# Layer 1's attention sums: the copy of W2's extra columns moved four rounds later in VectorE's order

## The chip, the cores and the metric

The kernel runs on one NeuronCore of a Trainium2 chip. The metric is the device time of one execution in microseconds (us). Before the change it is 1989.29 us, the median of three runs that took 1989.29, 1989.85 and 1982.86 us.

Names of engines: TensorE (PE in the profile, PEld for its weight loads), VectorE (DVE), ScalarE (ACT), GpSimd (POOL) and SyncE (SP). SyncE only issues DMA transfers here. GpSimd issues the indirect ones, which gather rows by a list of indices.

## What is computed

A pre-norm graph attention network with two layers on 3125 nodes of 768 values and 53125 edges (25000 drawn pairs in both directions and a loop at each node, sorted by destination). Layer 1 has 4 heads of 256 columns, layer 2 one head of 768. Cut to what matters:

```python
def gat_conv(x, edge_index, W, a_src, a_dst, bias, heads, out_ch, concat):
    xl = (x @ W).reshape(n, heads, out_ch)
    alpha_src = jnp.einsum('nhc,hc->nh', xl, a_src)
    alpha_dst = jnp.einsum('nhc,hc->nh', xl, a_dst)
    e = jax.nn.leaky_relu(alpha_src[src] + alpha_dst[dst], 0.2)
    m = jax.ops.segment_max(e, dst, num_segments=n)
    e = jnp.exp(e - m[dst])
    s = jax.ops.segment_sum(e, dst, num_segments=n)
    alpha = e / (s[dst] + 1e-16)
    out = jax.ops.segment_sum(xl[src] * alpha[:, :, None], dst, num_segments=n)
    ...
h0 = relu(layernorm(x))
h1 = relu(layer_norm(gat_conv(h0, W1, ...), g1, be1)) + (h0 @ Wr1 + br1)
h  = layer_norm(gat_conv(h1, W2, ...), g2, be2) + (h1 @ Wr2 + br2)
return x + h
```

## The kernel before

**Blocks.** The nodes are cut into 25 blocks of 128 destinations. The sorted edges of a block fill 17 tiles of 128 edges. A tile belongs to one or two quarters (32 destinations each) of its block.

**Layer 1's sums** (the function `sums`, called at the end of the stage with `first()` as an argument) compute the segment sum of messages. For each tile GpSimd gathers the 128 source rows of 1024 values from the DRAM table into a buffer `g` (L779, 512 KB), of which there are 13. VectorE makes the tile's weights `w` by two instructions: `oh`, a one-hot matrix of the destinations (L805), and `w`, that matrix times the attention factor of each head (L806). There are 9 buffers of the narrow `w` and 3 of the wide one. TensorE multiplies `w` by `g` into `pa` (L826).

**Rounds.** The 17 tiles of a block are taken in five rounds, 0 to 4, of 4, 4, 3, 3 and 3 tiles (three of these tiles lie in two quarters and have wide weights, so that every round is 16 products; the trace records each fp32 product twice, so a round is 32 records of L826). While TensorE works on a round, the gathers and weights of the next one are issued (`fetch`). After each round `step` runs once. It lets each generator in hand go one step further, up to its next `yield`: first `first()`, then the closing steps of finished blocks (`finish` and `end1`), then `more`, which fills gaps in TensorE's order with the residual products of later blocks (L1191, h0 times Wr1).

**The order.** PE, ACT and DVE run in the order in which this Python code emits their instructions (`manual_schedule`); GpSimd and SyncE have orders of their own. Every engine works through its instructions in order, so an instruction that waits holds all behind it.

**`first()`** closes the attention factors while the sums already run. `totals` transposes the factors, takes their running sums (the scan, L637), transposes back into `scr`, and stores the result to DRAM as `alo_d` (L642, 1700 KB, on SyncE's queue). Then `first()` takes a tile `w2` for layer 2's weights. It has the tag "W", as `scr` has, so it is the same memory, and whatever writes `w2` waits until the store has read `scr`. Eight transfers (L1214) bring W2 into columns 0 to 767 of `w2`, and a copy on VectorE (L1215) puts the two extra columns there: `wa2`, W2 times a_src2 and a_dst2, made long before. The names in the profile: w for `w2`, wa2s for `wa2`.

**Who else waits for the store.** Closing a block needs the totals of its last edges. They are fetched from `alo_d` by GpSimd (`ask`, L761, into `ao`), for block 0 behind the first gather of block 1's round 3, and for block 1 two gathers later. `finish` of block 0 starts on VectorE with L746, which reads `ao`, and goes on to `z` (L753, L1228), its layer norm (L486 to L1232) and, on TensorE, the transposes of `z` (L1239). `w2` itself is first read by the products for layer 2's table (L1260).

Of the kernel before, what the change touches and what calls it, by code (L numbers as in the profile page):

```python
# [69 lines left out]
def in_order(  # L70
# [170 lines left out]
    def edge_list(ep, pe):  # L241
# [32 lines left out]
        cnt = ep.tile([Q, NQ + 3], F32, name="cnt")  # L274
        first = ep.tile([Q, 1], I32, name="first")
        nc.vector.tensor_scalar(first, d_i[:, 0:1], 5, None, op0=OP.logical_shift_right)
        mark = ep.tile([Q, 6], F32, name="marks")
        for i in range(3):
            nc.vector.tensor_scalar(mark[:, i:i + 1], first, float(i + 1), None, op0=OP.add)
# [351 lines left out]
    def totals(heads, al, alo, alo_d, keep, xs, pp, tag, bufs):  # L631

        to_rows, to_slots = rows_and_slots(heads, pp, tag, bufs)
        for i, _ in enumerate(to_rows(al, xs)):
            if i == 1:
                yield
        nc.vector.tensor_tensor_scan(xs, keep[:, :S], xs, 0.0, op0=OP.mult, op1=OP.add)  # L637
        yield
        for i, _ in enumerate(to_slots(xs, lambda js, p: nc.scalar.activation(alo[:, js, heads:, :], p, AF.Copy))):
            if i == 1:  # L640
                yield
        nc.sync.dma_start(alo_d.rearrange("(p r) c -> p r c", p=128), alo.rearrange("p j v b -> p j (v b)"))  # L642
# [199 lines left out]
    with tc.tile_pool(name="m1", bufs=1) as mp:  # L842
# [322 lines left out]
        with tc.tile_pool(name="w2", bufs=1, reuse_waits="tile") as wp, tc.tile_pool(name="e1", bufs=2, reuse_waits="tile") as ep, \  # L1165
# [42 lines left out]
            def first():  # L1208
                nonlocal w2
                yield from totals(H, al1, alo1, alo1_d, keep1, xs1, pp, "p2", 2)  # L1210
                yield
                w2 = mp.tile([128, NK2, R2], F32, tag="W", name="w2")
                for k in range(NK2):
                    nc.sync.dma_start(w2[:, k, :C2], W2[k * 128:(k + 1) * 128, :])  # L1214
                nc.vector.tensor_copy(w2[:, :, C2:], wa2)  # L1215

            def end1(b, z, share):
# [50 lines left out]
                store_rows(nc.sync, table2, b, row)  # L1268

            sums(H, C1, table1, al1, alo1_d, 13, 3, gp, ap, pp, end1, more, (2.5, 3.8, 0, 0, 0.9), first(), -6.3)  # L1270


# [595 lines left out]
```

## Time and profile before

| | us |
|---|---|
| runs, median (lowest to highest) | 1989.29 (1982.86 to 1989.85) |
| profiled execution, its own time | 1990.46 |
| span of the profiled execution, first to last instruction | 1988.6 |
| PE busy in the span | 1793.4 (90%) |
| DVE busy in the span | 1060.1 (53%) |
| POOL busy in the span | 902.0 (45%) |
| granted TensorE clock, mean | 0.957 of full speed |

Times inside the trace are us from the start of the span. A row of a timeline has the start, the duration, the engine, the line, the operation, what it writes and reads, and the count of merged records; the brackets at its end give the engine's idle time just before and what ended it. "issue" stands for idle time in which the profile shows nothing that was waited for. A row of a table by stretch has the stretch, its length, the busy time of PE, PEld, DVE, ACT and POOL with the count of instructions, the granted clock, the mean busy share of the 16 DMA engines, and GB/s.

### The profile page before, as it was taken

The page shows a single profiled execution, that of the slowest core. Times are in us where ns is not written, and L with a number is a line of the kernel's source. Part 1 is how long each engine was busy: PE and PEld are TensorE (multiplying, and loading weights), DVE is VectorE, ACT ScalarE, POOL GpSimd, SP SyncE. Part 2 cuts the span into 40 slices and gives each one's busy share as a digit, 9 for nine tenths or more (in the row PEclk, how much of TensorE's full clock was granted, in tenths as well). Part 3 has the DMA queues.
Part 4 walks back from the last instruction along what each step waited for, and adds up shares of the span by engine and source line. Part 5 has one row for each costly group of instructions (what it writes and reads, how often), then busy time and mean ns, then how long its engine had stood idle before and what let it go on. Part 6 is the DMA issues. An engine that isn't in the chain of part 4 may idle for free. (4 is left out here: it accounts for less than half of the span.)

```text
span 1988.6 us, 34126 instructions
## 1 busy us (share of the span) xinstructions
PE 1793.4 (90%) x12558; PEld 985.9 (50%) x12558; DVE 1060.1 (53%) x3030; ACT 295.5 (15%) x1094; POOL 902.0 (45%) x977
## 2 busy tenths in 40 slices
PE   8999999998779999999998998838989888998986
PEld 5666665664446555565544554534333333333332
DVE  7673437886645555655566454524444444444445
ACT  2122331001211221221111211101000000000000
POOL 2000101112455566566656653052666666666662
PEclk9999999998889999999999999858999998999999
DMA  7823448774699999999999996486999999999984
GB/s 244 267 96 132 129 144 205 177 176 152 229 408 352 386 375 396 381 381 408 391 392 367 376 362 264 142 286 207 338 327 327 328 328 325 330 338 323 341 284 147
DMA packets 180786, 574.86 MB, mean 289 GB/s; under 512 B 32768, under 2 KB 55034, under 8 KB 180485
## 3 DMA queue, kind: packets, MB, share of 16 engines
q0 software_dynamic: 108432, 408.63, 57.5%
q1 hardware_dynamic: 67786, 153.57, 22.5%
q10 hardware_dynamic: 4394, 10.39, 1.3%
q8 instruction: 103, 1.69, 0.3%
q14 instruction: 71, 0.57, 0.1%
HBM read 503.27 MB, written 73.85 MB: 290 GB/s over the span
## 5 line engine op out<-in xcount | busy, mean ns | idle before, releaser
L779 POOL DMA_INDIRECT g<-table,idx_s x832 | 816.3, 981 | 555.6 <-issue 208.6
L826 PE MATMUL pa<-g,w 128*32 128x256 f32 (+2 forms) x5868 | 527.9, 429 | 69.5 <-issue 52.6
L826 PEld LDWEIGHTS pa<-g,w 128*32 128x32 f32 x5868 | 204.5, 111 | 360.8 <-issue 238.2
L1326 PE MATMUL pr<-wr,h 128*128 128x384 f32 (+1 forms) x800 | 299.2, 509 | 26.7 <-issue 26.3
L1260 PE MATMUL p<-w,h1T 128*128 128x384 f32 (+2 forms) x800 | 280.3, 497 | 5.2 <-DVE h1T L1246 2.6
L801 DVE TENSOR_SCALAR w<-iota_f,rel_s,al 128x32 f32<-128x32 f32 (+1 forms) x416 | 102.3, 318 | 264.1 <-PE pa L826 156.1
L1326 PEld LDWEIGHTS pr<-wr,h 128*128 128x128 f32 (+1 forms) x800 | 143.7, 190 | 182.1 <-issue 112.6
L1260 PEld LDWEIGHTS p<-w,h1T 128*128 128x128 f32 (+1 forms) x800 | 143.9, 187 | 127.8 <-issue 34.1
L806 DVE TENSOR_TENSOR w<-oh,al 128x128 f32<-128x128 f32 (+1 forms) x416 | 131.8, 317 | 124.8 <-PE pa L826 54.0
L931 PE MATMUL pm<-w,h0l 128*128 128x344 f32 (+1 forms) x468 | 144.2, 463 | 0.0
L1191 PE MATMUL pr<-h0k,wr 128*128 128x256 f32 (+1 forms) x576 | 141.8, 392 | 2.4 <-issue 2.2
L1068 PE MATMUL pm<-h0g,wr 128*128 128x512 f32 x288 | 134.2, 614 | 0.0
L931 PE MATMUL pm<-w,h0g 128*128 128x344 f32 x432 | 130.0, 456 | 0.3 <-ACT h0g L910 0.3
L1191 PEld LDWEIGHTS pr<-h0k,wr 128*128 128x128 f32 x576 | 106.3, 190 | 33.4 <-issue 13.0
L999 POOL DMA_DIRECT2D hot_d<-ohd x25 | 13.5, 540 | 222.7 <-DVE own L503 126.6
L805 DVE TENSOR_SCALAR oh<-iota_f,rel_s 128x32 f32<-128x32 f32 (+1 forms) x416 | 110.4, 265 | 0.5 <-issue 0.2
L492 ACT ACTIVATE bn_sd<-bn_mv,eps 128x1 f32<-128x1 f32 (+1 forms) x50 | 14.7, 294 | 638.6 <-DVE bn_mv L488 445.3
L931 PEld LDWEIGHTS pm<-w,h0l 128*128 128x128 f32 (+1 forms) x468 | 86.6, 189 | 45.7 <-issue 8.4
L931 PEld LDWEIGHTS pm<-w,h0g 128*128 128x128 f32 x432 | 81.4, 192 | 40.3 <-issue 0.9
L1068 PEld LDWEIGHTS pm<-h0g,wr 128*128 128x128 f32 x288 | 54.4, 197 | 58.0 <-issue 57.9
L552 PE MATMUL pq<-tabs,hot 128*128 128x25 bf16 x1275 | 41.7, 180 | 39.4 <-issue 35.5
L1244 ACT ACTIVATE h1T<-p,be_c,g_c 128x128 f32<-128x128 f32 (+1 forms) x200 | 72.0, 476 | 18.3 <-PE p L1239 12.6
(306 smaller groups left out, 1439.5 us busy)
## 6 DMA issues: line engine op xcount, KB each, us to landing
s<-slo_d SPq DMA_DIRECT2D x25, 544.0 KB
g<-table,idx_s POOLq DMA_INDIRECT x832
table<-row SPq DMA_DIRECT2D x24, 512.0 KB
own<-table SPq DMA_DIRECT2D x24, 512.0 KB
h1T_d<-h1T SPq DMA_DIRECT2D x24, 512.0 KB
h<-h1T_d SPq DMA_DIRECT2D x22, 512.0 KB
ring<-in_x_dram SPq DMA_DIRECT2D x24, 384.0 KB
table<-row SPq DMA_DIRECT2D x24, 384.0 KB
```

Source lines behind the costliest of these rows:

```text
L552: nc.tensor.matmul(q[:, j], oh[:P, o:o + 128], tabs[:, i], start=(i == 0), stop=(i == 2))
L779: nc.gpsimd.indirect_dma_start(out=g[:, :width], out_offset=None, in_=table[:, :], in_offset=bass.IndirectOffsetOnAxis(ap=idx_s[:, b * J + ...
L801: nc.vector.tensor_scalar(w[:, 0, :], iota_f[:, lo:hi], rel_s[:, c:c + 1], al[:, POS[j], 0, b:b + 1], op0=OP.is_equal, op1=OP.mult)
L805: nc.vector.tensor_scalar(oh, iota_f[:, lo:hi], rel_s[:, c:c + 1], None, op0=OP.is_equal)
L806: nc.vector.tensor_tensor(w, oh[:, None, :].to_broadcast([128, heads, hi - lo]), al[:, POS[j], :, b:b + 1].to_broadcast([128, heads, hi - ...
L826: nc.tensor.matmul(pa[32 * q:32 * q + 32, o // f, o % f:o % f + m], w[:, o // cols, :], g[:, o:o + m], start=to not in opened, stop=False, ...
L931: nc.tensor.matmul(pm[:r, :C], h0[b][:, k, :], w1[:, k, i * C:(i + 1) * C], start=(k == 0), stop=(k == NK1 - 1))
L1068: nc.tensor.matmul(pm, wr1[:, k, m * 128:(m + 1) * 128], groups[gi][:, k, :], start=(k == 0), stop=(k == NK1 - 1))
L1191: nc.tensor.matmul(pm[:, :n], wr1[:, k, m * 128:(m + 1) * 128], loaded[i, k][:, :n], start=(k == 0), stop=(k == NK1 - 1))
L1244: nc.scalar.activation(hT[:, k0 + k, :r], pt[:, k, :r], AF.Relu, bias=be1_c[:, k0 + k:k0 + k + 1], scale=g1_c[:, k0 + k:k0 + k + 1])
L1260: nc.tensor.matmul(pm[:, :n], hT[:, k, :r], w2[:, k, o:o + n], start=(k == 0), stop=(k == NK2 - 1))
L1326: nc.tensor.matmul(pm[:, :384], h1[:, k, :r], wr2[:, k, i * 384:(i + 1) * 384], start=(k == 0), stop=False)
```

## The change

`first()` yields four times between the loads of W2 and the copy:

```diff
                 for k in range(NK2):
                     nc.sync.dma_start(w2[:, k, :C2], W2[k * 128:(k + 1) * 128, :])
+                for _ in range(4):
+                    yield
                 nc.vector.tensor_copy(w2[:, :, C2:], wa2)
```

Since `first()` goes one step a round, the copy is emitted four rounds later. No engine but VectorE has another order, and the loads of W2 stay where they are on SyncE's queue. From the copy on, lines have numbers higher by 2, and the running numbers of the tiles `g` and `w` are lower by 1 between the two places.

VectorE's order before, at both places (`w_4678` is the last weight of block 1's round 0, `w_4711` the first of round 1, `w_4854` and `w_4860` the last two of round 4; L746 begins the closing of block 0; DMAHW5 is the semaphore of the store to `alo_d`):

```order
L806 TENSOR_TENSOR w_4678<-oh,al_120 128x128 [waits DVE_49,PE_49]
L1215 COPY w_4682<-wa2s 128x8x2 [waits DMAHW5_49,Activation_49]
L805 TENSOR_SCALAR oh<-iota_f,rel_s 128x32
L806 TENSOR_TENSOR w_4711<-oh,al_120 128x128 [waits DVE_49]
...
L806 TENSOR_TENSOR w_4854<-oh,al_120 128x128 [waits DVE_49,PE_49]
L805 TENSOR_SCALAR oh<-iota_f,rel_s 128x64
L806 TENSOR_TENSOR w_4860<-oh,al_120 128x256 [waits DVE_49]
L746 TENSOR_SCALAR aw<-ao,has 128x4 [waits DMASW4_49]
```

The same places in VectorE's order of the changed kernel:

```order
L806 TENSOR_TENSOR w_4678<-oh,al_120 128x128 [waits DVE_49,PE_49]
L805 TENSOR_SCALAR oh<-iota_f,rel_s 128x32
L806 TENSOR_TENSOR w_4710<-oh,al_120 128x128 [waits DVE_49,PE_49]
...
L806 TENSOR_TENSOR w_4853<-oh,al_120 128x128 [waits DVE_49,PE_49]
L805 TENSOR_SCALAR oh<-iota_f,rel_s 128x64
L806 TENSOR_TENSOR w_4859<-oh,al_120 128x256 [waits DVE_49]
L1217 COPY w_4682<-wa2s 128x8x2 [waits DMAHW5_49,Activation_49]
L746 TENSOR_SCALAR aw<-ao,has 128x4 [waits DMASW4_49]
```

The copy went behind the thirteen pairs L805 and L806 that make the weights of rounds 1 to 4 of block 1, and stands right ahead of block 0's closing. Its waits are the same.

GpSimd's order, which the change leaves as it is but for the tiles' numbers, here as the changed kernel has it (`g_4728` is the last gather of round 1, the next three are round 2, `g_4807`, `g_4815` and `g_4821` are round 3, `g_4845` begins round 4):

```order
L779 DMA g_4728<-table_64,idx_s 128x1024 [waits DMASW7_49,PE_49]
L779 DMA g_4761<-table_64,idx_s 128x1024 [waits DMASW0_49,PE_49]
L779 DMA g_4767<-table_64,idx_s 128x1024 [waits DMASW1_49,PE_49]
L779 DMA g_4773<-table_64,idx_s 128x1024 [waits DMASW2_49,PE_49]
L779 DMA g_4807<-table_64,idx_s 128x1024 [waits DMASW3_49,PE_49]
L761 DMA ao<-alo_d,at_last 128x200 [waits DMAHW5_49,DMASW4_49]
L779 DMA g_4815<-table_64,idx_s 128x1024 [waits DMASW5_49,PE_49]
L779 DMA g_4821<-table_64,idx_s 128x1024 [waits DMASW6_49,PE_49]
L761 DMA ao<-alo_d,at_last 128x200 [waits DMASW7_49]
L779 DMA g_4845<-table_64,idx_s 128x1024 [waits DMASW0_49,PE_49]
```

The first L761, of block 0, waits for the store to `alo_d` as the copy does, in both kernels.

## The prediction

> **What bounds the kernel now.** I began with the page, to see whether TensorE is the engine whose idle time counts, and then went to the place of the change with the view of who waited for whom, the timelines of the engines and a table of busy time by stretch. The page, whose second view cuts the span into 40 slices of 49.7 us:
>
> ```profile
> span 1988.6 us, 34126 instructions
> PE   8999999998779999999998998838989888998986
> PEclk9999999998889999999999999858999998999999
> DMA  7823448774699999999999996486999999999984
> ```
>
> TensorE is busy nine tenths of nearly every slice. Layer 1's sums start in slice 11 (about 520 us), and from there to about 1200 us the DMA engines are as full as TensorE is. The copy stands at 556 us, at the start of this stage. The waits between 520 and 640 us (us in total, times, longest):
>
> ```profile
> DVE w L1215 <- DMA alo_d<-scr: 14.7, 1, 14.7
> POOL ao L761 <- DMA alo_d<-scr: 7.7, 1, 7.7
> PE pa L826 <- DVE w L806: 6.6, 1, 6.6
> ```
>
> These three lines are the case. VectorE stands 14.7 us at the copy, until the store of scr to alo_d has read its buffer. Behind the copy stand weights w, and TensorE waits 6.6 us for the first of them. But GpSimd waits for the same store, at ask (L761), and what is queued there are the gathers g of the same sums. The change touches the first wait alone. So the question is what else TensorE would have waited for. The table by stretch (PE, PEld, DVE, ACT and POOL busy, then PEclk, DMA share, GB/s):
>
> ```profile
> 541.70:556.40 14.70, 7.46 (x68) 4.38 (x63) 0.00 (x0) 1.44 (x4) 4.68 (x5) 0.89 1.02 411
> 556.40:577.00 20.60, 16.04 (x124) 9.28 (x128) 15.49 (x53) 2.20 (x4) 13.45 (x14) 0.83 1.03 403
> 600.00:620.00 20.00, 20.00 (x128) 13.51 (x127) 5.91 (x21) 2.76 (x10) 7.32 (x8) 1.00 0.93 349
> 620.00:900.00 280.00, 276.34 (x2250) 163.84 (x2248) 162.12 (x539) 54.80 (x158) 171.50 (x180) 1.00 1.00 381
> ```
>
> TensorE is idle 7.2 us of the first stretch and 4.6 us of the second, and then hardly at all: 0 of 20 us and 3.7 of 280 us. Time that it has gained by 600 us would reach the end, since nothing later has slack to lose it in. Before 600 us the DMA engines are full (1.02 and 1.03 at over 400 GB/s) while TensorE has gaps: there the transfers set the pace.
>
> **The change part by part.** It removes and adds no instruction. On VectorE, thirteen pairs of L805 and L806, the weights of block 1's rounds 1 to 4, come ahead of the copy. VectorE's rows (start, us, idle before in brackets):
>
> ```profile
> 556.42 0.18 DVE L1215 COPY w<-wa2s 128x16 f32<-128x16 f32 x1 [14.74 <-DMA alo_d<-scr]
> 567.09 0.29 DVE L806 TENSOR_TENSOR w<-oh,al 128x128 f32<-128x128 f32 x1 [3.45 <-PE pr L1191]
> 567.93 0.33 DVE L746 TENSOR_SCALAR aw<-ao,has 128x4 f32<-128x4 f32 x1
> 576.18 0.81 DVE L1232 TENSOR_SCALAR z<-z,bn_mv,bn_rs 128x1024 f32<-128x1024 f32 x1
> ```
>
> The 14.74 us go: VectorE can write the weights from 541.7 us on. Does the copy wait at its new place? The pair before the last ahead of it is the row at 567.09, which waits for TensorE to free its buffer, held by round 1's weights. In the trace it is let go with the end of the L1191 matmuls behind round 1. Even if these end some us earlier, that is after 556.4, so the copy finds the store done, and the new wait is nil. The copy's own 0.18 us and a start of about 0.2 now lie ahead of block 0's z. z is finished at 577.0, and its reader L1239 starts at 585.06 (below), so 8 us hide these 0.4; without that cover they would cost 0.4 us. Now TensorE:
>
> ```profile
> 530.36 3.64 PE L826 MATMUL pa<-g,w 128*32 128x256 f32 x32
> 545.90 2.12 PE L826 MATMUL pa<-g,w 128*32 128x256 f32 x26 [1.06 <-issue]
> 547.95 2.86 PE L1191 MATMUL pr<-h0k,wr 128*128 128x256 f32 x12
> 557.45 5.16 PE L826 MATMUL pa<-g,w 128*32 128x256 f32 x32 [6.65 <-DVE w L806]
> 562.54 4.15 PE L1191 MATMUL pr<-h0k,wr 128*128 128x256 f32 x16
> 566.62 4.23 PE L826 MATMUL pa<-g,w 128*32 128x256 f32 x38
> 576.70 1.51 PE L826 MATMUL pa<-g,w 128*32 128x256 f32 x23 [1.69 <-DMA g<-table,idx_s]
> 583.24 1.89 PE L826 MATMUL pa<-g,w 128*32 128x256 f32 x26 [0.69 <-DMA g<-table,idx_s]
> 585.06 1.09 PE L1239 MATMUL p<-ident,z 128*128 128x128 f32 x8
> 595.28 1.93 PE L826 MATMUL pa<-g,w 128*32 128x256 f32 x32
> ```
>
> A round of the sums is 32 records. Round 1 of block 1 starts at 557.45, 6.65 us after L1191 ended at 550.81, and takes 5.16 us, since the first weights come one by one and the clock is halved. Without the copy the weights are there. Are the gathers? GpSimd's rows and the one of SyncE's queue that stores alo_d:
>
> ```profile
> 536.51 0.99 POOL L779 DMA_INDIRECT g<-table,idx_s  x1 [0.30 <-PE p L582]
> 542.58 0.94 POOL L779 DMA_INDIRECT g<-table,idx_s  x1 [1.31 <-PE p L582]
> 548.48 0.94 POOL L779 DMA_INDIRECT g<-table,idx_s  x1 [0.30 <-issue]
> 557.07 0.95 POOL L761 DMA_INDIRECT ao<-alo_d,at_last  x1 [7.66 <-DMA alo_d<-scr]
> 559.57 0.98 POOL L779 DMA_INDIRECT g<-table,idx_s  x1 [0.30 <-issue]
> 564.64 0.93 POOL L779 DMA_INDIRECT g<-table,idx_s  x1 [0.30 <-issue]
> 567.33 0.94 POOL L779 DMA_INDIRECT g<-table,idx_s  x1 [1.76 <-PE pr L1191]
> 571.05 1.07 POOL L779 DMA_INDIRECT g<-table,idx_s  x1 [0.30 <-issue]
> 618.00 0.93 POOL L779 DMA_INDIRECT g<-table,idx_s  x1 [8.85 <-PE pa L826]
> ```
>
> ```profile
> 543.55 0.32 SPq L642 DMA_DIRECT2D alo_d<-scr  x1
> ```
>
> By GpSimd's order 542.58 is the last gather of round 1, 559.57 that of round 3, 564.64 that of round 4, and 571.05 that of block 2's round 0. TensorE's two waits on gathers give their time under way: 564.64 to 576.70 is 12.1 us, 571.05 to 583.24 is 12.2 us. The store, issued 1 us behind round 1's last gather, took until 556.4, 12.9 us. From below: round 0's last gather, 536.51, was used from 545.90 at the latest, 9.4 us. So round 1's last gather lands between 552.0 (9.4) and 555.5 (12.9), and I take 554.7 (12.1), because it shares the engines with the store. Most of TensorE's 6.65 us is therefore hidden by nothing but changes its cause: 3.9 us stay as a wait for gathers, and 2.8 us are gained (2.0 to 5.4). The round then goes at the pace of the row at 530.36, which has the halved clock too: 3.64 for 5.16 us, 1.5 gained. TensorE is some 4.3 us ahead behind round 1 (3.5 to 6.9).
>
> It keeps none of this. Round 3's last gather is issued at 559.57, behind ask, and lands at about 571.7. Round 4's is issued at 564.64 and lands at 576.7, as in the row. All of GpSimd's gaps between 557.07 and 564.64 are its own 0.30 us: it runs at its own pace from the moment at which the store is done, and the change doesn't move the store. TensorE arrives 4 us earlier at the same two landings and waits there. What remains is GpSimd's first gather of block 2, which takes over a buffer of round 1: it waited 1.76 us, where the fourth gaps elsewhere are 1.31, so 0.45 us of it is TensorE's. With the DMA engines full, an issue that comes 0.45 us earlier lands between 0 and 0.45 us earlier. I take 0.2, about the middle.
>
> Sum: 14.7 us on VectorE, of which 4.3 reach TensorE, less 4.3 given back at rounds 3 and 4, plus 0.2: 0.2 us, or 1988.4 for the span of 1988.6. The profiled execution was timed at 1990.46, 1.9 above its span and 1.2 above the median of 1989.29. Against the median this is 1989.1, and I say **1989.0 us**: no change.
>
> **The rivals.** *First, the gain stays.* If the gathers are in SBUF when TensorE asks, it gains the whole 6.65 us, and round 1 runs in the 1.93 us of the row at 595.28 instead of 5.16, 3.2 more: 9.9 us, or 1979.4. For it: the trace names the weights as what ended the wait, and TensorE is full from 600 us on, so that a gain would last; 618.00 shows GpSimd waiting for TensorE, no longer the reverse. Against it: two waits on gathers stand between the copy and that point, and both are set by issues behind ask.
>
> *Second, slower: the clock.* TensorE's granted clock falls after a pause. Stretches of 3.41 us, columns as above:
>
> ```profile
> 549.79:553.20 3.41, 1.01 (x5) 0.56 (x3) 0.00 (x0) 0.62 (x2) 0.00 (x0) 1.00 1.01 424
> 553.20:556.61 3.41, 0.00 (x0) 0.00 (x0) 0.18 (x1) 0.00 (x0) 0.00 (x0) 0.50 0.99 408
> 560.03:563.44 3.41, 3.41 (x24) 2.01 (x15) 2.96 (x12) 0.00 (x0) 2.50 (x4) 0.50 1.03 394
> 570.27:573.68 3.41, 1.92 (x18) 0.83 (x21) 3.38 (x9) 0.10 (x1) 1.73 (x3) 1.00 1.03 405
> ```
>
> After a stretch with 1.01 us of work it was 0.50, and it stayed there to the end of a full stretch, 10.2 us in all. Between 570.27 and 573.68 TensorE still had 1.92 us of work, and kept its clock. When it arrives 4 us earlier, that work may be done before, the pause gathers around 570 to 576, and a second halved stretch of up to 10.2 us begins at 573.7, over work that is now at full clock. It costs one slow round at least (3.64 less 1.93, 1.7 us) and half the stretch at most, 5.1 us; with 3 us, 1992.3. It decides from the point at which a whole stretch has about 1 us of work. Against it: up to 583 us TensorE waits for gathers anyway, and these pauses would take up most of the loss.
>
> The Trainium skill (TensorE: Matmul & The Clock Gate, What's actually happening) has the same mechanism: the clock is halved after an idle window of about 3.4 us, and given back after a busy one. By that rule the pause moved to 570 us would halve the clock again if it covers a window; the rows agree on the length of a window, and none shows the pause there.
>
> *Third, the change does not take the wait away*: VectorE reaches the copy before the store is done and stands there again. That needs the L1191 matmuls behind round 1 to end before 556.4. At the earliest they end at 550.81 plus 1.93 for the round plus 3.8 for their 16 records (12 took 2.86), 556.5, with every gather there. So there is nothing left to wait for even then, and if there were, it would lie in z's 8 us of slack: 1989.3.
>
> **How the numbers follow.** No lasting effect, third rival included: 0.70. Gain stays, wholly or in half: 0.18. A second halved stretch: 0.12. A measurement can tell about 0.5% (9.9 us) from no change. The first rival just reaches that at its full size, which takes half its chance; with something that these rows do not show, 0.12 for faster. The second stays under 5.1 us, so slower by 0.5% needs a cause that I don't see: 0.08. Same: 0.80. The likeliest case alone spans what the three runs spanned, 1982.9 to 1989.9, and 1 or 2 us around it. The range takes in the first rival nearly whole and the second whole (1989.3 and 5.1 is 1994.4): 1980 to 1995.
>
> **What would show it.** Right: the copy at about 563 to 567 us with no idle time before it; VectorE's weights for rounds 1 and 2 before 550 us; TensorE's first matmuls of round 1 near 551, with a wait on gathers inside the round instead of one on w; and the waits on gathers near 576.7 and 583.2 still at the same times, the one at 576.7 longer than 1.69 us. Wrong: those two landings come several us earlier, so that they hung on TensorE or VectorE after all; or TensorE reaches them with its gathers there; or the clock reads 0.50 after 570 us, and the rows behind 588 us are later than now.

## The result and the profile after

The changed kernel takes 1984.35 us (median of 17 runs, 1979.03 to 1990.21), the kernel before 1987.07 us in 17 runs. The ratio is 0.9985, with a 95% interval from 0.9973 to 0.9997. A later set with the same two kernels gave 1.0009 (0.9995 to 1.0023). Taken together that is no change.

The profiled span went from 1988.6 to 1983.7 us, 4.9 us less, and nothing of this comes from the change. Here is the scan L637, which stands ahead of the change in VectorE's order, before and after:

```profile
530.78 4.69 DVE L637 TENSOR_TENSOR_SCAN scr<-keep,scr 100x2176 f32<-100x2176 bf16 x1 [7.40 <-ACT scr L573]
```

```profile
525.88 4.70 DVE L637 TENSOR_TENSOR_SCAN scr<-keep,scr 100x2176 f32<-100x2176 bf16 x1 [7.24 <-ACT scr L573]
```

The later trace is 4.90 us ahead before the changed code begins. So all times below are compared from the scan on. I call *the segment* the time from the scan's start to the gather behind GpSimd's wait of about 9 us, where TensorE is the bound again and nothing has slack: 618.00 less 530.78 is **87.22 us** before, 613.35 less 525.88 is **87.47 us** after. The change gains nothing in the place where it acts.

Inside the segment much moved. VectorE after (start, us, idle before):

```profile
542.10 0.29 DVE L806 TENSOR_TENSOR w<-oh,al 128x128 f32<-128x128 f32 x1 [2.95 <-remote]
545.22 0.29 DVE L806 TENSOR_TENSOR w<-oh,al 128x128 f32<-128x128 f32 x1 [1.39 <-PE pr L1191]
554.83 0.30 DVE L806 TENSOR_TENSOR w<-oh,al 128x128 f32<-128x128 f32 x1 [6.91 <-issue]
555.67 0.17 DVE L1217 COPY w<-wa2s 128x16 f32<-128x16 f32 x1
558.64 0.29 DVE L746 TENSOR_SCALAR aw<-ao,has 128x4 f32<-128x4 f32 x1 [2.80 <-DMA ao<-alo_d,at_last]
```

The copy has no idle time before it; the 14.74 us are gone. VectorE now waits in these four other places, 14.05 us in all ("remote" stands for a releaser that the profile does not tell). The longest wait, 6.91 us, is at the weight that takes over the buffer of round 1's first weight; the row names no releaser, but in VectorE's order this instruction waits for TensorE. The 2.80 us are for the totals. TensorE after (the rows of rounds 1 to 4, and the two waits on gathers in block 2's round 0):

```profile
545.99 1.05 PE L826 MATMUL pa<-g,w 128*32 128x256 f32 x4
550.71 0.59 PE L826 MATMUL pa<-g,w 128*32 128x256 f32 x2 [3.67 <-DMA g<-table,idx_s]
552.02 3.29 PE L826 MATMUL pa<-g,w 128*32 128x256 f32 x26 [0.72 <-DMA g<-table,idx_s]
555.24 3.72 PE L1191 MATMUL pr<-h0k,wr 128*128 128x256 f32 x16
558.89 1.64 PE L826 MATMUL pa<-g,w 128*32 128x256 f32 x23
560.90 0.39 PE L826 MATMUL pa<-g,w 128*32 128x256 f32 x1 [0.37 <-issue]
563.00 0.38 PE L826 MATMUL pa<-g,w 128*32 128x256 f32 x1 [1.71 <-issue]
565.12 0.58 PE L826 MATMUL pa<-g,w 128*32 128x256 f32 x1 [1.75 <-issue]
566.56 0.59 PE L826 MATMUL pa<-g,w 128*32 128x256 f32 x1 [0.86 <-issue]
568.01 6.08 PE L826 MATMUL pa<-g,w 128*32 128x256 f32 x69 [0.86 <-issue]
577.11 0.59 PE L826 MATMUL pa<-g,w 128*32 128x256 f32 x2 [0.68 <-DMA g<-table,idx_s]
578.39 1.89 PE L826 MATMUL pa<-g,w 128*32 128x256 f32 x26 [0.69 <-DMA g<-table,idx_s]
```

Round 1 begins 20.1 us after the scan instead of 26.7. It does two of its products and stops, for gathers: the wait of 6.65 us on w has become 3.67 and 0.72 us on g. The round ends 29.4 us after the scan (552.02 and 3.29, less 525.88), before it was 31.8.

Round 2 starts at 33.0 us (558.89; before 35.8) and breaks up: behind 23 of its 32 records come five gaps, 5.55 us together, for which the profile names no cause ("issue"). At 42.1 us (568.01) five of its records are still to come, and the lead is gone; before, TensorE was six records into round 3 at 40.1 us (566.62 and 4.23, less 530.78). Then rounds 3 and 4 go in one row without a wait. At the last gather of block 2's round 0 TensorE is at 52.5 us (578.39) in both traces (583.24 before). GpSimd after:

```profile
537.66 0.94 POOL L779 DMA_INDIRECT g<-table,idx_s  x1 [1.27 <-remote]
552.30 0.95 POOL L761 DMA_INDIRECT ao<-alo_d,at_last  x1 [7.79 <-DMA alo_d<-scr]
559.79 0.94 POOL L779 DMA_INDIRECT g<-table,idx_s  x1 [0.30 <-issue]
561.04 0.94 POOL L779 DMA_INDIRECT g<-table,idx_s  x1 [0.31 <-DMA g<-table,idx_s]
568.87 0.93 POOL L779 DMA_INDIRECT g<-table,idx_s  x1 [3.14 <-PE pa L826]
613.35 0.94 POOL L779 DMA_INDIRECT g<-table,idx_s  x1 [8.75 <-PE pa L826]
```

It still waits for the store at ask. Block 2's first gather (561.04) comes 35.2 us after the scan instead of 36.6, and its fifth (568.87) waits 3.14 us for TensorE and is back at 43.0 us, where it was (42.7; 573.50 before). The table by stretch after, with columns as in the prediction:

```profile
556.40:577.00 20.60, 14.35 (x116) 8.65 (x114) 11.71 (x38) 2.21 (x4) 12.64 (x14) 0.83 1.03 405
565.10:571.90 6.80, 5.05 (x40) 3.40 (x42) 3.01 (x10) 2.21 (x4) 3.05 (x4) 0.50 1.03 407
```

The DMA engines are as full as before (1.03 at 405 GB/s). The last row shows something new: the clock was halved a second time, from 565.1 to 571.9 us, over the end of round 2 and the first half of the row at 568.01, which is about round 3.

### The profile page after: what moved, and what is told of

It is laid out like the page before. It is cut to its first block, busy times and chain, and to the rows that moved or that the text cites. A ratio compares the mean times of both kernels' runs of the same rounds, so it can differ in the third digit from the quotient of the medians.

```text
span 1983.7 us, 34129 instructions
## 1 busy us (share of the span) xinstructions
PE 1797.1 (91%) x12558; PEld 988.9 (50%) x12558; DVE 1057.3 (53%) x3030; ACT 297.0 (15%) x1094; POOL 900.2 (45%) x977
## 5 line engine op out<-in xcount | busy, mean ns | idle before, releaser
L801 DVE TENSOR_SCALAR w<-iota_f,rel_s,al 128x32 f32<-128x32 f32 (+1 forms) x416 | 101.9, 315 | 255.2 <-PE pa L826 159.4
L806 DVE TENSOR_TENSOR w<-oh,al 128x128 f32<-128x128 f32 (+1 forms) x416 | 131.6, 316 | 136.5 <-PE pa L826 55.5
L1191 PE MATMUL pr<-h0k,wr 128*128 128x256 f32 (+1 forms) x576 | 141.9, 391 | 2.5 <-issue 2.3
L1068 PE MATMUL pm<-h0g,wr 128*128 128x512 f32 x288 | 132.7, 609 | 0.0
L1191 PEld LDWEIGHTS pr<-h0k,wr 128*128 128x128 f32 x576 | 105.6, 190 | 34.1 <-issue 14.2
L805 DVE TENSOR_SCALAR oh<-iota_f,rel_s 128x32 f32<-128x32 f32 (+1 forms) x416 | 108.6, 261 | 0.4
L1068 PEld LDWEIGHTS pm<-h0g,wr 128*128 128x128 f32 x288 | 53.6, 194 | 57.8 <-issue 57.5
L554 DVE TENSOR_TENSOR scr<-pq,ohh 128x500 f32<-128x500 f32 x100 | 56.8, 597 | 27.1 <-PE pq L552 27.0
```

Of the source, the lines that this page charges most:

```text
L554: nc.vector.tensor_tensor(pick[:, j0:j0 + n], q, ohh[:, j0:j0 + n, None, :].to_broadcast([128, n, heads, NB]), OP.mult)
L801: nc.vector.tensor_scalar(w[:, 0, :], iota_f[:, lo:hi], rel_s[:, c:c + 1], al[:, POS[j], 0, b:b + 1], op0=OP.is_equal, op1=OP.mult)
L805: nc.vector.tensor_scalar(oh, iota_f[:, lo:hi], rel_s[:, c:c + 1], None, op0=OP.is_equal)
L806: nc.vector.tensor_tensor(w, oh[:, None, :].to_broadcast([128, heads, hi - lo]), al[:, POS[j], :, b:b + 1].to_broadcast([128, heads, hi - ...
L1068: nc.tensor.matmul(pm, wr1[:, k, m * 128:(m + 1) * 128], groups[gi][:, k, :], start=(k == 0), stop=(k == NK1 - 1))
L1191: nc.tensor.matmul(pm[:, :n], wr1[:, k, m * 128:(m + 1) * 128], loaded[i, k][:, :n], start=(k == 0), stop=(k == NK1 - 1))
```

## Experiments

The runs were made in three sets, each timed beside the kernel before. Before took 1985.99 us in the first set, 1836.44 in the second and 1972.69 in the third, so times are compared within a set only. The segment is a difference inside one trace and is compared across all; each one is from the start of L637 to the gather behind the wait of 7 to 11 us, two rows of the run's timelines. The third column is the mean busy share of the DMA engines in the segment, and GB/s.

| run | segment, us | DMA share, GB/s | ratio to before (95% interval) |
|---|---|---|---|
| before, after | 87.22, 87.47 | 1.02 401, 1.02 401 | 0.9985 (0.9973 to 0.9997) |
| after_again | 87.26 | 1.02 402 | 1.0009 (0.9995 to 1.0023) |
| before_again | 87.45 | 1.03 405 | 1.0000 (0.9987 to 1.0013) |
| ask_late_copy_late | 88.11 | 1.01 398 | 1.0010 (0.9992 to 1.0027) |
| ask_late_copy_old | 87.41 | 1.02 400 | 0.9993 (0.9979 to 1.0007) |
| loads_late | 87.32 | 1.02 396 | 1.0007 (0.9991 to 1.0024) |
| loads_twice | 97.13 | 1.02 400 | 1.0053 (1.0035 to 1.0072) |
| loads_half | 84.13 | 1.03 405 | 0.9991 (0.9978 to 1.0003) |
| loads_half_copy_old | 83.84 | 1.03 405 | 0.9970 (0.9955 to 0.9986) |
| old_wait0 | 87.89 | 1.02 399 | 0.9992 (0.9972 to 1.0012) |
| old_wait3 | 94.21 | 0.98 372 | 1.0043 (1.0025 to 1.0061) |
| old_wait7 | 101.64 | 0.90 345 | 1.0076 (1.0047 to 1.0106) |
| late_wait3 | 92.04 | 0.98 381 | 1.0014 (0.9993 to 1.0036) |

**Is there a gain at all?** The two kernels unaltered:

> The changed kernel once more, unaltered. The segment is the time from the start of the scan L637 to the gather behind GpSimd's wait of about 8.8 us, where TensorE is the bound again: 87.2 us in the profile before (530.78 to 618.00), 87.5 in the profile after (525.88 to 613.35). Theory (gathers behind ask set the pace, so the copy gives at most 0.5 us): segment 86.5 to 88, ratio to before 0.9990 to 1.0010. Rival (the copy's place is worth the 2.7 us between the medians): segment 84 to 86, ratio 0.998 to 0.999.

> The kernel before once more, unaltered, to see how far the segment (scan L637 to the gather behind GpSimd's wait of about 9 us) differs between executions of one kernel. Theory (the transfers set the segment's length): 86.7 to 87.9, as in the six traces so far (87.2 to 88.1). Rival (the copy's place counts and the traces met it by chance): a segment more than 1 us away from 87.3.

Four segments of the two kernels lie between 87.22 and 87.47, with the copy early in two of them and late in two. The rival, that the 2.7 us between the first medians are the copy's, falls: after_again has the other sign, and no segment is near 84 to 86.

**What holds the segment: the order behind ask, or the bytes?** First ask itself, with the copy late:

```diff
-                if heads > 1 and b == 1 and place == 11:
-                    ask(0)
-                if heads > 1 and b and place == (13 if tiles_of(b) == J else 5):
+                if heads > 1 and b == 1 and place == 16:
+                    ask(0)
+                    ask(1)
+                if heads > 1 and b > 1 and place == (13 if tiles_of(b) == J else 5):
                     ask(b)
```

> The changed kernel with both fetches of totals (ask of blocks 0 and 1) moved behind the last gather of block 1, so that no gather of rounds 3 and 4 stands behind the store in GpSimd's order. Theory (gathers behind ask set the pace): these gathers are issued about 7 us earlier, TensorE's waits in rounds 3 and 4 shrink, and the segment is 2 to 6 us shorter than after's 87.5; ratio 0.996 to 0.999. If the DMA engines rather than the issue hold the gathers, they land no earlier and the segment stays at 87 to 88. Rival (the copy's wait alone counted): segment as after, 87 to 88.

> The kernel before, copy at its old place, with both fetches of totals moved behind the last gather of block 1. Theory (two covers, each hides the other): the copy's wait of about 14 us stays and TensorE starts round 1 when the store is done, but finds the gathers of rounds 3 and 4 earlier: segment 1 to 4 us shorter than 87.2, and 1 to 4 us longer than with the copy late; ratio 0.998 to 1.000. Rival (the copy alone counts): segment 87 to 88, ratio 1.000.

With the copy late, round 3's last gather was issued at 550.55 and round 4's at 557.80, 20.90 and 28.15 us after the scan; after has them at 554.81 and 559.79, 28.93 and 33.91. So the issue did come 8.0 and 5.8 us earlier, and the segment did not get shorter (88.11); with the copy at its old place it was 87.41, where 1 to 4 us less than 87.2 were expected. Two rows of TensorE and one of VectorE tell where it went (with the copy late):

```profile
573.62 3.18 PE L827 MATMUL pa<-g,w 128*32 128x256 f32 x28 [1.69 <-DMA g<-table,idx_s]
580.60 3.29 PE L827 MATMUL pa<-g,w 128*32 128x256 f32 x29 [2.74 <-DVE oh L806]
574.18 0.29 DVE L746 TENSOR_SCALAR aw<-ao,has 128x4 f32<-128x4 f32 x1 [14.45 <-DMA ao<-alo_d,at_last]
```

TensorE still waits for the last gather of round 4, which now has been under way for 15.8 us (557.80 to 573.62) instead of some 12. It can go on at 44.0 us after the scan, before at 45.9: an issue 5.8 us earlier is worth about 2 us at the landing. Then TensorE waits 2.74 us for block 2's weights, since VectorE stood 14.45 us at the totals that are now fetched later. So my statement that the landings are set by the issues behind ask was at best half of it. And since moving ask brings this new wait, these two runs alone don't show whether the order or the bytes hold the segment.

Then the loads of W2, at the copy's new place and from ScalarE's queue:

```diff
+                for _ in range(4):
+                    yield
                 for k in range(NK2):
-                    nc.sync.dma_start(w2[:, k, :C2], W2[k * 128:(k + 1) * 128, :])
-                for _ in range(4):
-                    yield
+                    nc.scalar.dma_start(w2[:, k, :C2], W2[k * 128:(k + 1) * 128, :])
                 nc.vector.tensor_copy(w2[:, :, C2:], wa2)
```

> The changed kernel with the eight loads of W2 (3.1 MB, some 7.7 us of the DMA engines at 405 GB/s) issued from ScalarE's queue at the copy's new place instead of from SyncE's queue as soon as the store is done. Theory (the DMA engines are full, so what is queued ahead of the gathers decides when they land): gathers of rounds 3 and 4 land 3 to 7 us earlier though they are issued at the same time, and the segment is 2 to 6 us shorter than 87.5; ratio 0.996 to 0.999. If the issue behind ask decides alone, the segment stays at 87 to 88. Rival (copy alone): as after.

The queue's row and the stretch in which the loads were missing, from this run:

```profile
566.48 6.42 ACTq L1216 DMA_DIRECT2D w<-in_L_gnn_W_dram  x7
```

```profile
557.00:566.00 9.00, 5.33 (x36) 2.51 (x35) 7.06 (x22) 0.07 (x1) 6.52 (x7) 0.95 0.93 309
```

The loads moved by some 15 us on the segment's scale (the first of them, issued just ahead of this row, at 566.07, 40.3 us after the scan; in before it was at 556.46, 25.7 us). In their absence the DMA engines moved 309 GB/s instead of the 401 that after shows between the same times, with GpSimd only just issuing again behind ask; then the loads took their share later. The expected 2 to 6 us did not come. The same bytes still had to pass within the segment, which would explain it. To see that it is the bytes, their number was changed, up and down (both against the changed kernel):

```diff
-                for k in range(NK2):
+                for k in list(range(NK2)) * 2:
                     nc.sync.dma_start(w2[:, k, :C2], W2[k * 128:(k + 1) * 128, :])
```

> The changed kernel with the eight loads of W2 issued twice into the same tile: 3.1 MB more for the DMA engines in this place and nothing else. Theory (the bytes between the scan and layer 2's first products set the segment's length): at 405 GB/s 7.8 us more, some of which the 8.8 us wait of GpSimd at the end may take up, so segment 91 to 95.5 and ratio 1.002 to 1.004. Rival (GpSimd's issue behind ask sets it, at its own 1.24 us a gather): segment 87 to 88.5, ratio 1.000.

```diff
-                for k in range(NK2):
+                for k in range(NK2 // 2):
                     nc.sync.dma_start(w2[:, k, :C2], W2[k * 128:(k + 1) * 128, :])
                 for _ in range(4):
                     yield
+                for k in range(NK2 // 2, NK2):
+                    nc.scalar.activation(w2[:, k, :C2], wr1[:, k - NK2 // 2, :C2], AF.Copy)
```

> The changed kernel with only four of the eight loads of W2; the other half of the tile is filled by ScalarE from the weights Wr1 that lie in SBUF, so layer 2's table is computed with other weights. 1.57 MB fewer, 3.9 us of the DMA engines at 405 GB/s. Theory (bytes): segment 83.5 to 86, ratio 0.9980 to 0.9995. Rival (GpSimd's issue): 87 to 88.

> The kernel before (copy at its old place) with the same half of the loads of W2 and the same fill by ScalarE. If the transfers still cover the copy's wait: segment within 0.5 us of the run with half the loads and the copy late. If half the loads uncover it: 1 to 3 us longer than that run. Rival (GpSimd's issue decides both): both 87 to 88.

In the last of these runs the copy stands ahead of the four yields, at its old place. With half of the loads ScalarE fills the other half of `w2` from Wr1, so what layer 2 computes is other numbers with the same work. The gather that ends the segment with the loads twice, and with half of them (their scans start at 519.16 and 517.04):

```profile
616.29 0.94 POOL L779 DMA_INDIRECT g<-table,idx_s  x1 [8.87 <-PE pa L826]
```

```profile
601.17 0.94 POOL L779 DMA_INDIRECT g<-table,idx_s  x1 [8.80 <-PE pa L826]
```

3.1 MB more make the segment 9.7 us longer, 1.57 MB fewer make it 3.3 us shorter. Both are near the bytes' time at 405 GB/s, 7.8 and 3.9 us. The first is 1.9 us above it, and above the expected range. By the third column, times the segment, 38.9 MB passed with the loads twice, 35.4 in before_again of the same set: 0.3 MB more than the loads account for, at 400 instead of 405 GB/s, which makes up the 1.9 us. The share in that column is 1.01 to 1.03 in every run down to old_wait0: the DMA engines are full over nearly all of the segment, and its length follows the bytes. This settles what holds the segment: the bytes that must pass in it. With half the loads the copy's place is still worth nothing there: 83.84 us with the old place, 84.13 with the new one, though VectorE stood 16.31 us at the old one. The timed medians of these two differ by 3.9 us in favour of the old place (1829.94 and 1833.82); 0.3 us of this lies in the segment, and where the rest lies was not followed.

**How much cover has the old place?** In the last set VectorE was made to stand longer: one copy more, which reads two values of one of the loads and so waits for that load; what it writes is overwritten.

```diff
+                nc.vector.tensor_copy(w2[:, 0, C2:], w2[:, 0, :2])
                 nc.vector.tensor_copy(w2[:, :, C2:], wa2)
```

(with 3 and 7 for 0 in the next two runs, and 3 at the copy's new place, in the changed kernel, in the last).

> The kernel before with one more copy on VectorE ahead of the old one. It reads two values of the first of W2's eight loads and is then overwritten, so that VectorE stands at the old place until that load has landed, by my estimate some 6 us after the store. This lengthens the wait of 14.7 us that the change removes. Theory (the transfers give TensorE 7.9 us of slack between 556 and 600 us: 4.6 and 3.3 in the table by stretch): hidden, segment 87 to 88.5 (87.2 and 87.5 in the two traces of before). Rival (what VectorE waits there reaches the end): 6 us more, 93.

> The same with the fourth load, by estimate some 12 us after the store. Theory: beyond the 7.9 us of slack, so 3 to 6 us show: segment 90 to 93.5, ratio 1.0015 to 1.003. Rival (whatever VectorE waits there is hidden): 87 to 88.5.

> The same with the last load, by estimate some 20 us after the store. Theory: 10 to 14 us show: segment 97 to 102, ratio 1.005 to 1.008. Rival (hidden): 87 to 88.5.

> The changed kernel with the same extra copy on the fourth load, so the wait stands at the copy's new place. Theory: the weights of rounds 1 to 4 are ahead of it, block 0's z has some 8 us of slack, so it is hidden: segment 87 to 88.5, and against the run with the same wait at the old place 2 to 6 us are gained: the move would be worth what its cover lacks. Rival (the place never matters): both runs alike.

VectorE's extra copy and TensorE's wait behind it, with the first load:

```profile
559.38 0.17 DVE L1215 COPY w<-w 128x2 f32<-128x2 f32 x1 [21.13 <-DMA w<-in_L_gnn_W_dram]
560.53 4.26 PE L826 MATMUL pa<-g,w 128*32 128x256 f32 x32 [13.10 <-DVE w L806]
```

and with the fourth:

```profile
569.65 0.17 DVE L1215 COPY w<-w 128x2 f32<-128x2 f32 x1 [27.59 <-DMA w<-in_L_gnn_W_dram]
570.74 4.20 PE L826 MATMUL pa<-g,w 128*32 128x256 f32 x32 [17.77 <-DVE w L806]
```

With 21.13 us on VectorE, TensorE's wait doubles (13.10 for 6.65 us), and the segment is 87.89: hidden but for half a microsecond. With 27.59 it is 94.21, 0.7 us above the expected range, and with the last load, at 35.12 us, 101.64. From the run with the fourth load to the one with the last the wait grows by 7.5 us and the segment by 7.4: beyond the cover each us counts in full. Drawn back from there, the cover ends at about 20.8 us on VectorE, 6 us above the 14.74 that the change removes; 7.9 had been read from TensorE's idle time. Beyond the cover the third column falls, to 0.98 and 0.90: the waiting TensorE frees no gather buffers, GpSimd issues no gathers, and the DMA engines run dry. In old_wait7 GpSimd waits 16.66 us for TensorE (whose first product behind its own wait is at 573.40), and the stretch ahead of the end of that wait is nearly empty of transfers:

```profile
577.45 1.12 POOL L779 DMA_INDIRECT g<-table,idx_s  x1 [16.66 <-PE pa L826]
```

```profile
570.00:575.00 5.00, 1.59 (x9) 0.64 (x13) 2.25 (x11) 0.00 (x0) 0.00 (x0) 0.50 0.10 37
```

The transfers moved 37 GB/s there.

The last run missed its expectation: 8.46 us of waiting at the new place, and the segment is 92.04 instead of 87 to 88.5. The extra 4.6 us lie in one round, block 2's round 1. In before it is the row

```profile
587.81 2.44 PE L826 MATMUL pa<-g,w 128*32 128x256 f32 x32
```

and in this run it begins at the same distance from the scan (57.2 for 57.0 us) and goes in pieces until 592.4:

```profile
585.23 1.67 PE L826 MATMUL pa<-g,w 128*32 128x256 f32 x19
...
591.49 0.92 PE L826 MATMUL pa<-g,w 128*32 128x256 f32 x4 [0.80 <-issue]
592.34 5.09 PE L1191 MATMUL pr<-h0k,wr 128*128 128x256 f32 x16
```

TensorE was on time up to there, so VectorE's wait did not reach it through the weights before. What ended the gaps the profile does not say ("issue"). Gaps of this kind, like those in round 2 of after, stand in the segments of all ten traces of the result and of the first and third set, 2.1 to 7.9 us a trace, 4.2 in before and 7.9 in after, and in none of the four traces of the second set. So they need not come from the copy's place. There is one trace of this run, and its timed ratio (1.0014, 0.9993 to 1.0036) allows 0 as well as 4.6 us. Whether the new place is worse covered than the old one stays open.

No version among these beats both kernels: the only shorter segments are those with half of W2 left out.

## Why the prediction was right

**The place.** That the copy holds VectorE and TensorE, and that another wait stands right behind, was read correctly: 6.65 us on w became 4.39 us on gathers (3.67 and 0.72), where 3.9 were forecast.

**The new wait of the copy**, nil, was right, with a smaller margin than thought. The weight buffer ahead of it was let go at the end of round 1 (554.83), ahead of the L1191 matmuls (555.24), and the copy ran 3.4 us after ask, which waits for the same store, could start (552.30). On the scale of before that is 560.6, earlier than the forecast 563 to 567. The weights of round 2 were written by 550.4 on that scale, just past the forecast 550.

**TensorE's lead behind round 1** was the mis-sized term: 4.3 us (3.5 to 6.9) were forecast, 2.4 measured. Its first part, 2.8 us from an earlier landing of the gathers (12.1 us under way, 9.4 to 12.9), is at fault: it was worth 0.5 us. The last gather of the round was issued at 537.66 and used at 552.02, 14.4 us, outside the bounds. A likely reason, which no run separates, is that it shares the engines with the 1.7 MB of the store. The second part, the round's own pace, was forecast at 3.64 us and took 3.29 from the last landing on. Since the whole lead is given back, the error did not reach the sum.

**Given back** was right in amount, and half wrong in how. The lead was to go in waits on the gathers of rounds 3 and 4. In after it goes in the gaps of round 2 that the profile does not explain, and TensorE passes rounds 3 and 4 without a wait on a gather, which the prediction had named as a sign of being wrong. The forecast wait on the last gather of round 4 would have been there for a faster TensorE: the trace's semaphore records have this landing at 572.04 or later, 46.2 us after the scan, and in before TensorE waited for it until 45.9. That is an argument; two runs of the second set, which has no such gaps, show it. With half of W2's loads and the copy late, then with the copy at its old place (scans at 517.04 and 513.63):

```profile
544.86 3.46 PE L826 MATMUL pa<-g,w 128*32 128x256 f32 x26 [0.84 <-DMA g<-table,idx_s]
556.54 2.37 PE L826 MATMUL pa<-g,w 128*32 128x256 f32 x28 [1.67 <-DMA g<-table,idx_s]
560.52 0.59 PE L826 MATMUL pa<-g,w 128*32 128x256 f32 x2 [1.61 <-DMA g<-table,idx_s]
562.60 3.63 PE L826 MATMUL pa<-g,w 128*32 128x256 f32 x28 [1.49 <-DVE w L806]
```

```profile
541.87 5.16 PE L826 MATMUL pa<-g,w 128*32 128x256 f32 x32 [4.58 <-DVE w L806]
551.06 4.65 PE L826 MATMUL pa<-g,w 128*32 128x256 f32 x66
558.95 3.19 PE L826 MATMUL pa<-g,w 128*32 128x256 f32 x28 [1.65 <-DMA g<-table,idx_s]
```

The copy late ends round 1 at 31.3 us after the scan, the old place at 33.4: 2.1 us of lead. Then TensorE waits 1.67 and 1.61 us for gathers in rounds 3 and 4 and 1.49 us for weights, where with the old place it runs through round 3 (the row of 66 records), and the last 28 records of round 4 begin at 45.6 and 45.3 us. Here the lead is given back in rounds 3 and 4, mostly to gathers, as the prediction had it.

As to what sets these landings, I put them down to the issues behind ask, on the ground that GpSimd runs at its own 0.30 us gaps from there. The runs with ask late show that an issue 6 to 8 us earlier gives about 2 us at the landing, and none in the segment. What holds the segment is the other thing that the prediction named, the full DMA engines; the runs with more and fewer bytes show it.

**The remainder**, 0.2 us gained, was 0.25 us lost in the two traces, and 0.2 is also what two traces of one kernel differ by. That the forecast of 1989.0 us stands 4.7 above the measured 1984.35 says nothing of the mechanism: 2.2 us of it are the median of the kernel before, 1989.29 in three runs and 1987.07 in 17, and the rest is of the size by which the two sets differ.

**The rivals.** The full gain did not occur. The second, a further halved stretch of the clock, did: 6.8 us from 565.1 on. It had no price that the segment shows. Round 3 went slower, and TensorE still arrived at the gathers of block 2's round 0 before they landed (0.68 and 0.69 us of waiting). That the pauses would take up most of the loss was the argument against it, and it held. The two halved stretches of after each follow a window with little work (columns as in the table):

```profile
548.04:551.45 3.41, 0.59 (x2) 0.14 (x2) 0.00 (x0) 0.00 (x0) 0.00 (x0) 1.00 1.00 414
551.45:554.86 3.41, 2.84 (x25) 1.48 (x26) 0.03 (x1) 0.00 (x0) 1.94 (x3) 0.50 1.03 412
561.69:565.10 3.41, 0.38 (x1) 0.12 (x2) 3.20 (x9) 0.00 (x0) 2.50 (x4) 1.00 1.02 393
```

The first shrank from 10.2 us to one window, in which TensorE worked 2.84 us; the second comes behind the gaps of round 2. By the rule of the Trainium skill (TensorE: Matmul & The Clock Gate, What's actually happening), an idle window halves the clock and a busy one gives it back. The trace agrees, but for windows that were not wholly idle: 0.59 and 0.38 us of work were little enough.

The third rival did not occur.

## What to carry to other kernels

A long wait that the profile names is worth only what lies between it and the next wait behind: here 14.7 us on one engine were 6.6 on the engine that counts, and none at the next point where the bytes of the transfers had to be through. To price a wait, lengthen it: a stall that can grow by 6 us without effect has nothing to give. And compare two traces from a point ahead of the change: here the whole difference of the spans had come about before it.

## What was not expected of the hardware

Two executions of the same code ahead of the change differ by 4.9 us in 530. Of these, 2.8 us come about in the last 70 us ahead of the scan, before and after, each from the start of the same row of TensorE (L1068):

```profile
458.31:530.78 72.47, 54.16 (x295) 30.49 (x296) 43.57 (x51) 13.54 (x19) 18.70 (x19) 0.85 0.46 160
```

```profile
456.23:525.88 69.65, 52.37 (x299) 29.94 (x300) 43.54 (x50) 13.48 (x19) 18.58 (x19) 0.88 0.48 166
```

The same work had a clock of 0.85 and of 0.88. Halved stretches that fall on other work from one execution to the next would do this; no run here tests it.

The kernel before took 1986, 1836 and 1973 us in the three sets. In the second, layer 2's sums are the largest part of what is shorter: VectorE makes their weights (L801) from 1368.4 to 1973.2 us in the trace of before and from 1305.1 to 1815.1 in that of before_again, which is 95 of the 156 us between the two spans. Stretches out of this stage, before_again first:

```profile
1330.00:1800.00 470.00, 451.74 (x2553) 189.96 (x2551) 248.97 (x758) 45.52 (x402) 359.70 (x363) 1.00 1.00 380
```

```profile
1340.00:1950.00 610.00, 545.31 (x3014) 228.16 (x3012) 271.66 (x811) 52.60 (x433) 382.17 (x386) 0.96 0.89 316
```

The transfers of that stage ran at 380 GB/s in one and 316 in the other, with one program. Why, no run here shows. The segment, with its 401 and 405 GB/s, has the same length in both (87.22 and 87.45 us).
